# Local attention: the full-row products issued just ahead of the step's first MLP unit, the division ahead of the residual additions

## The chip, the cores and the metric

The kernel runs on one core of a Trainium2 chip. The metric is the device time of one execution in microseconds; the times are medians of several runs. One further execution is recorded by the hardware profiler, and everything that is read from the profile comes from that execution.

## What is computed

Eight sequences of 1024 rows and 256 columns, all in f32, go through two parts, each with a layer norm ahead of it and a residual addition behind it. The first part is a latent attention with 16 heads. The second part is a network of two layers, and the change lies in it:

```python
for l in range(2):
    h = shift_token(x)                       # right half of the columns one row down
    q, k, v = split(h @ wqkv[l])             # 8 heads of 64
    q, k = rotary_xpos(l2norm(q) * qs, l2norm(k) * ks)
    # windows of 128 rows; a query sees its own window and the one before,
    # at most 128 keys back
    o = softmax(mask(8 * q @ k.T)) @ v
    x = x + o @ wo[l]
    h = layernorm(shift_token(x)) * ln_g[l] + ln_b[l]
    a, g = split(h @ w1[l] + b1[l])          # 682 columns each
    x = x + (a * gelu(g)) @ w2[l] + b2[l]
```

## The kernel before, in words

The first part fills the first third of the time, the function `local` the rest. In `local` a pass is one layer of one sequence; there are 16 passes (8 sequences in layer 0, then 8 in layer 1), each of 8 windows of 128 rows, so 128 windows. One loop over steps starts a window per step and runs the parts of earlier windows beside it. The order on PE, DVE, ACT and POOL is the order in which this loop issues (a manual schedule); SP, which issues the DMAs, is ordered by the scheduler.

A step issues, by name: `qk` of this window (PE: 32 matmuls of 512 columns into the tile `pair`; ACT squares; DVE `t1`, `t2`, two operations on `ss`; POOL adds, takes an inverse root and multiplies); `transposes` of the window before (DVE into `turned`, stores to DRAM `z`, and the load `qkT`); `values` of the window four back; `v` of this window (PE: tile `pv`; ACT copies it to `lv`); an output that was held (below); a unit of the MLP; `halves` of the window four back; `scores` of the window three back (PE into `pair`; ACT takes exponentials into `pt`, which POOL masks with one or two selections for each half of the heads); what is left of the MLP's second product (`rests`); `divide` of the window four back (DVE, and for odd windows the DMAs `zo` and `oT`); the output of two windows, every second step; and a second unit of the MLP.

The products of the exponentials with v are made in two parts. `values` (L1068) issues the full-row ones: 128 rows, 32 columns of the array, 65 columns moved, 64 of them (32 for window 0, which has no window before it). `halves` issues, at the same line, those in which only half the rows of a block count. Both add into two PSUM tiles `o`: one has the bank of the pool `pacc`, the other is one of the three banks of the pool `psum3` (tag "mm"), which it holds until `divide` has read it. The other users of these three banks are `pv`, the output's `psw` (L1120, read by the addition at L1124), the MLP's up products `ag` (L724; a gelu on ACT at L1215 reads the gate, a multiplication on DVE at L1216 the other) and its down products `psy`, two tiles, each read by an addition at L1253 (and L1259 in layer 1).

An MLP chunk of 512 rows has eight units and two are run in a step, so the steps repeat in fours. They are named here by their units:

- held step: hidden slices 0 and 1; an output that was held goes ahead of its unit
- middle step: hidden slices 2 and 3; an output at its end
- closing step: hidden slice 4, and the remainder, with statistics and transposes for the next chunk
- sums step: the down products `psy`, 160 matmuls, whose remainder (`rest`, 32 matmuls with 64 rows) and additions follow the scores; then the scaling of the next chunk

Only in the sums step is `rests` filled when the step comes to it. Its output is then put on `held` and issued in the next step. A window with number 2 or 6 starts in a sums step, 3 or 7 in a held step, 0 or 4 in a middle step, 1 or 5 in a closing step.

Within a held, middle or closing step, PE thus runs qk, full-row products, v, (held output), up products, halves, scores, (output), up products.

Of the kernel before, what the change touches and what calls it, by code (L numbers as in the profile page):

```python
# [83 lines left out]
def preln_mla_local_kernel(  # L84
# [627 lines left out]
    def local(ctx: ExitStack, verdict):  # L712
# [39 lines left out]
        def load_attention(l):  # L752


            w = {}
            queue = nc.sync if l else nc.scalar
            w["qkv"] = wa.tile([P, 2, 3 * INNER], F32, tag="qkv", name=f"l_qkv{l}")
            nc.sync.dma_start(w["qkv"], wqkv[l].rearrange("(c p) e -> p c e", p=P))

            for name, src in (("cos", xpos_cos), ("sin", xpos_sin)):  # L760
                w[name] = wa.tile([P, NT, 2, DH], F32, tag=name, name=f"l_{name}{l}")
                queue.dma_start(w[name], src)
                f = wa.tile([P, 2, DH], F32, tag=f"f{name}", name=f"l_f{name}{l}")
                for i, sc_ in enumerate((q_scale, k_scale)):
                    if name == "cos":
                        queue.dma_start(f[:, i, :], sc_[l].partition_broadcast(P))
                    else:
                        queue.dma_start(f[:, i, :H], sc_[l, H:].partition_broadcast(P))
                        queue.dma_start(f[:, i, H:], sc_[l, :H].partition_broadcast(P))
                w[f"f{name}"] = f  # L770
            return w

        def scale_tables(w):
            for name in ("cos", "sin"):
                f = w[f"f{name}"].unsqueeze(1).to_broadcast([P, NT, 2, DH])
                nc.vector.tensor_tensor(w[name], w[name], f, ALU.mult)

        def load_o(l):

            w = wa.tile([P, 4, D], F32, tag="o", name=f"l_o{l}")  # L780
            nc.sync.dma_start(w, wo[l].rearrange("(c p) e -> p c e", p=P))
            return w
# [357 lines left out]
        rests, held = [], []  # L1140
# [135 lines left out]
        def ahead(n):  # L1276
            if n < len(passes):
                l, b = passes[n]
                if n not in streams:
                    streams[n] = stream(b, l)  # L1280
                return next(streams[n])
# [10 lines left out]
        def each(step, name, back):  # L1292
            j = step - back
            if 0 <= j < windows:
                n, i = divmod(j, NT)
                getattr(made[n], name)(i)
# [6 lines left out]
        with tc.manual_schedule(engines={E.PE, E.DVE, E.Activation, E.Pool}):  # L1303
            for step in range(windows + LAG):
                n, i = divmod(step, NT)
                if step < windows and i == 0:
                    l, b = passes[n]
                    if n and b == 0:
                        o = w["o"]
                        w = load_attention(l)  # L1310
                        w["o"] = o
                    made[n] = Pass(n, l, b, w, *ready.pop(n))
                late = step < windows and n and i == 0 and b == 0
                if not late:
                    each(step, "qk", 0)
                each(step, "transposes", 1)
                each(step, "values", 4)
                if not late:
                    each(step, "v", 0)
                while held:  # L1320
                    j = held.pop()
                    made[j // NT].output(j % NT // 2)
                if step >= LAG:
                    next(units, None)
                if NT - 2 <= i and step < windows:
                    ahead(n + 1)
                each(step, "halves", 4)
                if 0 <= step - 3 < windows:
                    nc.scalar.activation(spark, column, AF.Exp)
                each(step, "scores", 3)  # L1330
                full = bool(rests)
                while rests:
                    rests.pop()()
                each(step, "divide", 4)
                if step >= 4 and (step - 3) % LOOK == 0 and step - 4 < windows:
                    inverses = stats.rearrange("p n r h -> p (n r h)")
                    ok = p1.tile([P, INNER], F32, tag="on", name=f"okl{step}")[:, : LOOK * HEADS]
                    nc.vector.tensor_scalar(ok, inverses, 1 / LOW, None, ALU.is_le)
                    nc.vector.scalar_tensor_tensor(ok, inverses, 1 / HIGH, ok, ALU.is_ge, ALU.mult)
                    verdict.add(ok, "local")  # L1340
                j = step - 6
                if 0 <= j < windows and j % 2 == 0:
                    if full and step + 1 < windows:
                        held.append(j)
                    else:
                        made[j // NT].output(j % NT // 2)
                elif 0 <= j < windows - 1 and (j + 1) % (B * NT) == 0:
                    w["o"] = load_o(passes[(j + 1) // NT][0])
                if step >= LAG - 2:
                    next(units, None)  # L1350
                if late:
                    scale_tables(w)
                    each(step, "qk", 0)
                    each(step, "v", 0)
                if i >= NT - 5 and step < windows:
                    got = ahead(n + 1)
                    if got:
                        ready[n + 1] = got
                while rests:
                    rests.pop()()  # L1360
            for _ in units:
                while rests:
                    rests.pop()()
# [519 lines left out]
    with ExitStack() as two:  # L1883
        local(two, verdict)
# [89 lines left out]
```

## Time and profile before

| | |
|---|---|
| median of three runs | 3241.62 us (3237.79 to 3249.9) |
| the profiled execution | 3238.44 us, its span 3236.6 us |
| PE busy | 3082.1 us, 95% |
| DVE busy | 2365.7 us, 73% |
| ACT busy | 1707.0 us, 53% |
| POOL busy | 1375.4 us, 42% |
| full-row products, 128 x 32 array | 7680 matmuls, busy 149.7 us |
| products of half rows | 7680 matmuls, busy 107.1 us |
| division: L1088, L1089, L1096 on DVE | 43.5, 108.6 and 91.1 us |
| additions of psy at L1253 on DVE | 42.7 us for 64 |

A line of a timeline begins with the start and the duration of a group of like instructions in us, then engine, source line, operation, output and input tile, shapes and count; in brackets stands the idle time of the engine before it and what ended it. A line of the waits gives the waiting engine, line and tile, what it waited for, and us in total, times, longest. A line of a table of stretches gives the stretch, its length, the busy time of PE, weight loads (PEld), DVE, ACT and POOL with their counts, PE's granted clock, the share of the DMA engines and GB/s. Matmuls are pipelined: a busy PE may hold products that wait.

### The profile page before, as it was taken

The numbers are of one execution on the slowest core, as the hardware profiler recorded it, in microseconds if no ns is written. First come the engines' busy times: TensorE is split into PE (matmuls) and PEld (weight loads), VectorE is DVE, ScalarE is ACT, GpSimd is POOL, SyncE is SP. The second block draws the span as 40 slices with busy tenths as digits, with TensorE's granted clock in tenths as the row PEclk, the third lists the DMA queues.
The fourth block names the chain that finished last, engine by engine and source line by source line (L and its number), as shares of the span: only waits on it lengthen the run. The fifth ranks groups of instructions, "written<-read, shape, count | busy, mean of one in ns | idle before, by whom it ended". The sixth has DMA issues, their size and how long they took to land. (4 is left out here: it accounts for less than half of the span.)

```text
span 3236.6 us, 124318 instructions
## 1 busy us (share of the span) xinstructions
PE 3082.1 (95%) x55618; PEld 1488.2 (46%) x55618; DVE 2365.7 (73%) x3761; ACT 1707.0 (53%) x2114; POOL 1375.4 (42%) x1070
## 2 busy tenths in 40 slices
PE   7999999999876999999999998999999999999998
PEld 2344444444323555455554444544445455554453
DVE  5999999999875767777676766666666776666652
ACT  6888989888521444444444443334444444444441
POOL 1011111111075655555555554555555555556540
PEclk9999999999998999999999999999999999999999
DMA  5343333333335455554655546555655556565451
GB/s 137 77 103 95 98 101 92 100 93 96 119 109 142 131 163 151 146 158 152 167 141 161 158 133 177 156 155 174 171 156 159 160 158 165 163 177 148 144 154 55
DMA packets 457517, 444.86 MB, mean 137 GB/s; under 512 B 179551, under 2 KB 390926, under 8 KB 456846
## 3 DMA queue, kind: packets, MB, share of 16 engines
q1 hardware_dynamic: 454990, 434.42, 48.2%
q8 instruction: 438, 7.18, 0.9%
q10 hardware_dynamic: 1984, 2.41, 0.2%
q14 instruction: 105, 0.86, 0.1%
HBM read 207.38 MB, written 174.56 MB: 118 GB/s over the span
## 5 line engine op out<-in xcount | busy, mean ns | idle before, releaser
L483 DVE TENSOR_TENSOR pt<-pt,er 128x1024 f32<-128x1024 f32 x576 | 676.0, 1219 | 32.0 <-ACT pt L469 27.0
L724 PE MATMUL ag<-d,l 128*32 128x512 f32 x5632 | 649.7, 595 | 15.1 <-ACT ge L1215 11.1
L958 POOL TENSOR_TENSOR t<-t,t 128x1024 f32<-128x1024 f32 x128 | 303.7, 2373 | 796.4 <-DVE t L954 796.4
L469 ACT ACTIVATE pt<-sc 128x1024 f32<-128x1024 f32 x576 | 560.1, 1029 | 94.2 <-PE sc L461 78.1
L724 PE MATMUL pair<-l_qkv,xT 128*32 128x512 f32 x4096 | 473.0, 595 | 4.4 <-ACT pt L1020 2.6
L1020 ACT ACTIVATE pt<-pair 128x1024 f32<-128x1024 f32 (+1 forms) x256 | 235.5, 968 | 363.7 <-PE pair L1014 357.7
L127 POOL TENSOR_TENSOR rn<-ss,half 128x16 f32<-128x16 f32 x128 | 372.8, 2913 | 13.7
L724 PEld LDWEIGHTS ag<-d,l 128*32 128x32 f32 x5632 | 184.0, 110 | 387.3 <-issue 334.0
L496 PE MATMUL acc<-pt,v 128*32 128x512 f32 (+3 forms) x3072 | 330.7, 500 | 7.4 <-DVE pt L483 7.1
L423 POOL TENSOR_SCALAR_AFFINE_SELECT er<-er 128x128 f32<-128x128 f32 x64 | 74.6, 1175 | 600.9 <-ACT er L421 600.0
L1068 PEld LDWEIGHTS o<-lv,pt 128*32 128x32 f32 (+1 forms) x15360 | 224.4, 108 | 198.3 <-issue 167.3
L949 ACT ACTIVATE sq<-pair 128x1024 f32<-128x1024 f32 x128 | 131.0, 1024 | 347.5 <-issue 326.6
L1216 DVE SCALAR_TENSOR_TENSOR hid<-ag,l_b,ge 128x512 f32<-128x512 f32 x160 | 117.4, 734 | 268.1 <-PE ag L724 175.6
L951 DVE TENSOR_TENSOR t<-pair,l_cos 128x1024 f32<-128x1024 f32 x128 | 155.3, 1213 | 200.7 <-ACT sq L949 200.2
L1120 PE MATMUL psw<-l_o,oT 128*32 128x256 f32 x4096 | 249.7, 395 | 41.8 <-DMA oT<-zo 30.3
L724 PE MATMUL psy<-l,hid 128*32 128x256 f32 x5120 | 284.1, 379 | 0.0
L1068 PE MATMUL o<-lv,pt 128*32 128x65 f32 (+1 forms) x15360 | 256.8, 223 | 20.1 <-POOL pt L1022 12.0
L982 DVE STREAM_TRANSPOSE turned<-t 128x512 f32<-128x512 f32 x256 | 166.0, 685 | 146.1 <-DMA zh<-turnedh 82.4
L724 PEld LDWEIGHTS pair<-l_qkv,xT 128*32 128x32 f32 x4096 | 132.6, 110 | 303.4 <-issue 283.7
L724 PEld LDWEIGHTS psy<-l,hid 128*32 128x32 f32 x5120 | 243.2, 110 | 46.2 <-issue 14.8
L461 PE MATMUL sc<-q,k 32*128 32x512 f32 (+3 forms) x3072 | 248.5, 380 | 12.9 <-DVE x L576 6.8
L724 PE MATMUL pv<-l_qkv,xT 128*32 128x512 f32 x2048 | 252.6, 598 | 0.0
(261 smaller groups left out, 4187.5 us busy)
## 6 DMA issues: line engine op xcount, KB each, us to landing
z<-turned SPq DMA_DIRECT2D x512, 128.0 KB
qkT<-z SPq DMA_DIRECT2D x128, 512.0 KB
zo<-ot SPq DMA_DIRECT2D x256, 128.0 KB
oT<-zo SPq DMA_DIRECT2D x64, 512.0 KB
y<-xs SPq DMA_DIRECT2D x128, 128.0 KB
h<-y SPq DMA_DIRECT2D x32, 512.0 KB
zx<-turneds SPq DMA_DIRECT2D x120, 128.0 KB
xT<-zx SPq DMA_DIRECT2D x240, 64.0 KB
```

The lines of the kernel that those rows point to most:

```text
L127: nc.gpsimd.tensor_tensor(out_, in_, half[:, :n], ALU.pow)
L461: nc.tensor.matmul(two[n // 2][:, n % 2, lo : lo + w], k[rows], q[rows, h], start=(h == 1), stop=(h == 0),)
L469: nc.scalar.activation(pt, sc, AF.Exp, scale=SCALE)
L483: nc.vector.tensor_tensor(t, t, er.to_broadcast([P, 1024 // w, w]), ALU.mult)
L496: nc.tensor.matmul(self.acc[g][32 * n : 32 * n + 32, q0 - c * 512 :], self.v[:, kb, h * VW - at : h * VW - at + 32], pts[n // 2][:, n % 2, ...
L724: nc.tensor.matmul(out[four], w[:, four], rhs, start=start, stop=stop)
L951: nc.vector.tensor_tensor(t1, qk, A[:, i].unsqueeze(2).to_broadcast([P, 2, HEADS, DH]), ALU.mult)
L958: nc.gpsimd.tensor_tensor(t1, t1, t2, ALU.add)
L982: nc.vector.transpose(t[:, :, n], r[:, n])
L1020: nc.scalar.activation(pt[:, :, : n * P], flat[:, :, : n * P], AF.Exp, scale=-1.0)
L1068: nc.tensor.matmul(o[r][32 * c : 32 * c + 32, 2 * g + h % 2, :], self.pts[m][g][rows, place(j), q0 : q0 + 32], self.vs[m][rows, h, :], sta ...
L1120: nc.tensor.matmul(ps[four, i, :], oT[:, (s + 2 * c) % 4, i, c, :], self.w["o"][:, c, :], start=c == 0, stop=c == 3,)
```

## The change

`values` of a step is issued behind `v` and behind a held output, just ahead of the step's first unit, where it stood ahead of both. And `divide` (with the check of its sums, every 32 steps) is issued ahead of the remainder of the down products and their additions, where it stood behind them. No instruction is added or removed.

```diff
                 if not late:
                     each(step, "qk", 0)
                 each(step, "transposes", 1)
-                each(step, "values", 4)
                 if not late:
                     each(step, "v", 0)
                 while held:
                     j = held.pop()
                     made[j // NT].output(j % NT // 2)
+                each(step, "values", 4)
                 if step >= LAG:
                     next(units, None)
...
                 each(step, "scores", 3)
-                full = bool(rests)
-                while rests:
-                    rests.pop()()
                 each(step, "divide", 4)
                 if step >= 4 and (step - 3) % LOOK == 0 and step - 4 < windows:
...
                     verdict.add(ok, "local")
+                full = bool(rests)
+                while rests:
+                    rests.pop()()
                 j = step - 6
```

## The prediction

> **What bounds the kernel now.** The page first, for the engine that carries the time; then the stretch of the local stage in which window steps and MLP units run side by side (1063 to 3094 us).
>
> ```profile
> PE 3082.1 (95%) x55618; PEld 1488.2 (46%) x55618; DVE 2365.7 (73%) x3761; ACT 1707.0 (53%) x2114; POOL 1375.4 (42%) x1070
> ```
> ```profile
> 1063.00:3094.00 2031.00, 1976.46 (x40908) 1020.81 (x40900) 1384.02 (x2486) 873.65 (x1034) 1128.82 (x834) 0.99 0.56 158
> ```
>
> PE is busy for 1976 of 2031 us at a clock of 0.99, so an order that leaves its work as it is can win only PE's waits there: at most some 55 us, and those inside a row of waiting products, which counts as busy. The waits, for this stretch, show which there are:
>
> ```profile
> PEld o L1068 <- POOL pt L1022: 14.0, 39, 1.4
> PE psw L1120 <- DMA oT<-zo: 12.7, 5, 4.8
> PEld ag L724 <- DVE xs L1124: 11.9, 12, 1.0
> PE ag L724 <- ACT ge L1215: 11.1, 14, 0.8
> PE o L1068 <- DVE stats L1088: 4.0, 4, 3.1
> ```
>
> Only the first and the last touch the moved products (o, L1068). The totals of PEld overlap PE's work, so I took the loss from the starts in the timeline. A closing step, and the sums step that follows such a step:
>
> ```profile
> 1927.71 1.10 PE L1068 MATMUL o<-lv,pt 128*32 128x65 f32 x64
> 1928.62 1.90 PE L724 MATMUL pv<-l_qkv,xT 128*32 128x512 f32 x16
> ```
> ```profile
> 1520.26 1.47 PE L1068 MATMUL o<-lv,pt 128*32 128x65 f32 x62
> 1521.03 0.64 POOL L1027 TENSOR_SCALAR_AFFINE_SELECT pt<-pt 128x512 f32<-128x512 f32 x1
> ...
> 1521.56 0.23 PE L1068 MATMUL o<-lv,pt 128*32 128x65 f32 x2
> 1521.62 1.89 PE L724 MATMUL pv<-l_qkv,xT 128*32 128x512 f32 x14
> 1523.26 8.88 PE L724 MATMUL psy<-l,hid 128*32 128x256 f32 x160
> ```
>
> Undisturbed, 64 full-row products take 0.91 us and v 1.72 us (start of pv to start of what follows). In the sums step both take 3.00 instead of 2.63 us: the last products wait for the second mask of the step before, which ends at 1521.67. The step before is the shortest (13.3 us), so POOL has not caught up.
>
> **The change, part by part.** *Nothing added:* the built programs have the same instructions on each engine; PE's order, and with it the PSUM banks, differ, DVE's division and additions are exchanged, ACT and POOL keep their order, and SP's queue swaps one load with two stores, once, near the end of the kernel. So no instruction is priced, only waits.
>
> *Full products behind v (and behind the held output).* They start 1.72 us later (5.17 us in a held step). In the sums step above they would start at about 1521.98, after the mask's end. Reading every step of the stretch in this way (time from the start of qk to pv, less the undisturbed 4.35 us): the 29 sums steps lose 0.33 to 0.38 us each, one of them 2.31, of which 1.72 can be hidden: 28 x 0.36 + 1.72 = 11.8 us. Three of the closing steps lose 0.34: 1.0 us. Middle steps lose nothing. Held steps with window 7 lose 0.03 to 0.73, 5.1 us in twelve steps (one more lost 3.3 us inside qk and one spans the change of layer; both are left out):
>
> ```profile
> 1539.48 0.60 PE L1068 MATMUL o<-lv,pt 128*32 128x65 f32 x26 [0.41 <-POOL pt L1022]
> ...
> 1545.05 1.96 PE L724 MATMUL ag<-d,l 128*32 128x512 f32 x16
> 1547.80 1.92 PE L724 MATMUL ag<-d,l 128*32 128x512 f32 x16 [0.79 <-ACT ge L1215]
> ```
>
> The wait of 0.79 stays: in both programs the second up product of that unit has the bank of the first, and waits for its gelu. Held steps with window 3 gain nothing: there the second up product waits for the addition of psw on DVE, whose chain from the end of qk (square 1.0, t1 1.2, t2 1.3, two ss 2.5, transposes 1.3, addition 0.65, some 0.2 between) is 8.15 us, against 7.8 us of PE's work whatever its order. Sum: 17.9 us.
>
> *What is queued behind, and the covers.* Behind the moved products stands the step's unit, then halves and scores. v's copy on ACT starts earlier, never later. The held output now goes ahead of the products, so a late oT would hold both; but oT lands 8.0 to 14.5 us before that psw in each of the 29 steps, and psw moves up by only 0.9 us. v's bank in the held step now comes from the division of the sums step, psw's and the products' from the two additions behind it.
>
> *Division ahead of the additions.* It acts in sums steps alone, where units leave a rest. DVE stands idle until psy is ready, with the division behind it:
>
> ```profile
> 2816.28 0.69 DVE L1253 TENSOR_TENSOR xs<-psy,xs 128x512 f32<-128x512 f32 x1 [1.44 <-PE psy L724]
> ...
> 2819.38 0.17 DVE L1088 RECIPROCAL stats<-o 128x4 f32<-128x4 f32 x1
> ```
>
> The division needs only halves, which end before scores and rest. Its 1.9 us (two reciprocals 0.17, two multiplications 0.42, a transpose 0.71) move into idle time, of which the waits list 30.7 us in 21 cases. PE waits for that division for only 4.0 us, already in the losses of the held steps, so I add nothing. Where DVE had no idle time (layer 0, window 6: 1533.79 to 1539.7 without a gap), the additions come 1.9 us later instead; the first would end at about 1537.6 and psw, whose bank it frees, starts at 1540.0: 2.4 us of cover. SP's store of xs waits as long, ahead of a qkT load whose scores come two steps later.
>
> *What is late next.* Only psw at the end of a middle step, which waits for oT of the held step before. For window 0 (13 steps in the stretch) the landing precedes its use by 0.1 to 2.4 us, and in five PE waits already (read from the starts: 1.0, 1.5, 1.7, 1.9 and 3.8 us). In layer 0 the chain behind that oT goes through DVE and SP's queue and does not get earlier, so the gain ahead of it (about 0.9 us: 0.36 + 0.43) is lost in two cases wholly and in one by half: +2 us. In layer 1 the chain gets earlier with the division.
>
> *Ahead of 1063 us* there is no MLP, and the products waited 17.0 us in all by the same rows (PE 7.3, PEld 9.7). Bounds: 0, as halves follow at once and oT's landing (11.1 us there) is next, to 4 x 1.72 = 6.9 us for the four steps with a long wait. I take 3, nearer to 0, because those steps end in waits for DMAs.
>
> Sum: -17.9 + 2 - 3 = -19 us (-0.6%). The profiled execution took 3238.44 us (span 3236.6), 3.2 us under the median of 3241.62. 3241.62 - 19 gives 3223 us.
>
> **Rivals.** *Absorbed:* what the products give back is waited for elsewhere, as in the window-3 steps. For it: every held step has a wait behind the products. Against it: in the sums step nothing behind them (psy, halves, scores) waits. It would leave the closing steps and half of what the sums steps lose: -7 us, 3235.
>
> *Slower, by the exchange on DVE.* The additions free the banks of psw and of the products in the held step, and now stand behind 1.9 us of division. Where the first addition ends later than 1.72 us after qk, PE waits. For it: layer 0, window 6, where DVE is full. Against it: the cover of 2.4 us above, and 3.5 us in layer 1. If the cover were missing in 16 held steps the price is 16 x 1.9 = 30 us, less 19: +11, 3253. It decides when DVE runs over 2.4 us later than in this trace.
>
> *Slower, by the clock.* PE gets ahead of oT; a long wait is followed by half clock:
>
> ```profile
> 2142.80 6.56 PE L1120 MATMUL psw<-l_o,oT 128*32 128x256 f32 x64 [3.74 <-DMA oT<-zo]
> ```
> ```profile
> 2141.90:2148.70 6.80, 5.90 (x56) 3.16 (x60) 3.68 (x8) 0.00 (x0) 2.55 (x5) 0.50 0.40 66
> ```
>
> The same psw takes 3.7 us elsewhere; 6.8 us at half clock cost 3.4. The other four waits (1.0 to 1.9 us) kept the full clock, and 0.9 us more leaves them under 3.74. If eight of the 13 went cold: 8 x (3.4 + 0.9) = 34 us, less 19: +15, 3257.
>
> The Trainium skill, "TensorE: Matmul & The Clock Gate", section "HAM oscillation — how this bites in real kernels", has the rule that PE gaps above about 3.4 us cost the clock. The one wait of 3.74 us agrees, the shorter ones do too; by the rule the forecast stands unless a wait for oT grows past that length.
>
> *More:* with DVE earlier, the additions of psw and oT come earlier too: two thirds of the 11.9 us and the 4 us of waits for oT in layer 1 go as well, about -31, 3211.
>
> **Chances.** Forecast 0.70 (its own range 3213 to 3232, from the bounds of the early steps and a few us of PE waits without a releaser that move from run to run); absorbed 0.10; the two slower ones 0.08 and 0.06; more 0.06. A measurement of this kernel can tell 0.5%, 16 us, from no change. Of the forecast's 0.70, 0.51 lies beyond that and 0.19 within; with the rivals: faster 0.57, within 0.29, slower 0.14. The range leaves out the slower cases and the far end of the last: 3204 to 3244.
>
> **What would show it.** Right: in sums steps the products take 0.91 us, none of L1068 waits for POOL pt in the stretch, qk to the unit stays at 6.07 us, the additions (L1253) hardly wait, and the 0.79 us for ge and the 8.15 us chain remain. Wrong: psw waiting for L1253, rows of 0.50 clock at psw, or sums steps as long as before (18.06 and 17.81 us).

## The result and the profile after

The changed kernel takes 3232.45 us (median of 20 runs, 3222.03 to 3246.82) against 3245.79 us for the kernel before in the same comparison (20 runs, 3237.22 to 3262.77): a ratio of 0.9963, 95% interval 0.9949 to 0.9977, so about -12 us (-17 to -7). A second comparison (12 runs, with the experiments below) gave 0.9982 (0.9963 to 1.0001), -6 us. It is faster, by less than the forecast's -19 us. Its profiled execution took 3227.63 us, the span 3225.9.

The page, and the stretch of the step loop in which window steps and MLP units run side by side, cut so that it holds the same 115 steps as the stretch shown of before. The stretch begins at the step that is called the first MLP step here and in the expectations, though the step ahead of it already runs up products:

```profile
PE 3073.7 (95%) x55618; PEld 1406.1 (44%) x55618; DVE 2362.0 (73%) x3761; ACT 1707.8 (53%) x2114; POOL 1371.3 (43%) x1070
```
```profile
1068.90:3083.70 2014.80, 1962.63 (x40904) 935.73 (x40900) 1380.91 (x2488) 873.58 (x1033) 1124.91 (x833) 0.99 0.57 159
```

The same 115 steps took 2030.3 us before (1063.92 to 3094.20) and take 2014.8 us now: 15.5 us less. But the stretch begins at 1068.8 in place of 1063.9, so 4.9 us were lost ahead of it (the expectations say 5.0). Behind it nothing differs (142.4 and 142.3 us). The waits of the stretch that answer to those shown of before:

```profile
PEld ag L724 <- DVE xs L1124: 14.7, 14, 1.3
PE psw L1120 <- DMA oT<-zo: 13.4, 8, 3.4
PE ag L724 <- ACT ge L1215: 12.4, 15, 1.1
PE pv L724 <- DVE on L1089: 3.3, 2, 2.1
DVE stats L1088 <- PE o L1068: 3.0, 6, 1.1
DVE xs L1253 <- PE psy L724: 2.9, 4, 0.9
PEld o L1068 <- POOL pt L1022: 0.5, 1, 0.5
PE o L1068 <- POOL pt L1022: 0.4, 1, 0.4
```

The products' waits for POOL are all but gone (14.0 and 3.6 us before, 0.5 and 0.4 now). The additions, which waited 30.7 us in 21 cases, wait 2.9 us in four. Two of these lines of before, which the prediction does not show:

```profile
PE o L1068 <- POOL pt L1022: 3.6, 7, 1.3
DVE xs L1253 <- PE psy L724: 30.7, 21, 4.4
```

New are two waits of v for the division: v has the bank that the division of the sums step sets free. The waits of psw for oT are more in number (8, were 5).

A sums step behind a closing step, on PE, and the second mask of the step before on POOL:

```profile
1525.64 0.64 POOL L1027 TENSOR_SCALAR_AFFINE_SELECT pt<-pt 128x512 f32<-128x512 f32 x1
```
```profile
1526.59 1.10 PE L1068 MATMUL o<-lv,pt 128*32 128x65 f32 x64
1527.51 8.81 PE L724 MATMUL psy<-l,hid 128*32 128x256 f32 x160
```

The mask ends at 1526.28; the products start 0.31 us later, in one row of 64, and take 0.92 us from start to start. Undisturbed sums steps fell from 18.05 to 17.62 us (window 6) and from 17.81 to 17.39 us (window 2).

In the held step that follows, the gelu's wait is what it was, and in layer 1 the division now stands ahead of the additions on DVE with no gap between them:

```profile
1552.90 1.92 PE L724 MATMUL ag<-d,l 128*32 128x512 f32 x16 [0.79 <-ACT ge L1215]
```
```profile
2806.70 0.14 DVE L1088 RECIPROCAL stats<-o 128x4 f32<-128x4 f32 x1
...
2807.89 0.71 DVE L1096 STREAM_TRANSPOSE ot<-on 128x512 f32<-128x512 f32 x1
2808.53 0.65 DVE L1253 TENSOR_TENSOR xs<-psy,xs 128x512 f32<-128x512 f32 x1
```

### The profile page after: what moved, and what is told of

Same layout as the page of the kernel before. It is cut to its first block, busy times and chain, and to the rows that moved or that the text cites. A ratio compares the mean times of both kernels' runs of the same rounds, so it can differ in the third digit from the quotient of the medians.

```text
span 3225.9 us, 124287 instructions
## 1 busy us (share of the span) xinstructions
PE 3073.7 (95%) x55618; PEld 1406.1 (44%) x55618; DVE 2362.0 (73%) x3761; ACT 1707.8 (53%) x2114; POOL 1371.3 (43%) x1070
## 5 line engine op out<-in xcount | busy, mean ns | idle before, releaser
L724 PE MATMUL ag<-d,l 128*32 128x512 f32 x5632 | 647.6, 594 | 15.2 <-ACT ge L1215 12.4
L724 PEld LDWEIGHTS ag<-d,l 128*32 128x32 f32 x5632 | 176.8, 109 | 348.1 <-issue 294.2
L1215 ACT ACTIVATE ge<-ag,l_b 128x512 f32<-128x512 f32 x160 | 110.1, 688 | 289.3 <-PE ag L724 284.7
L1068 PE MATMUL o<-lv,pt 128*32 128x65 f32 (+1 forms) x15360 | 245.4, 222 | 4.6 <-POOL pt L1022 4.3
```

Source lines behind the costliest of these rows:

```text
L724: nc.tensor.matmul(out[four], w[:, four], rhs, start=start, stop=stop)
L1068: nc.tensor.matmul(o[r][32 * c : 32 * c + 32, 2 * g + h % 2, :], self.pts[m][g][rows, place(j), q0 : q0 + 32], self.vs[m][rows, h, :], sta ...
```

## The experiments

The timed comparisons differ by a few us between runs of one kernel, so each profile was also read in the same way: the start of the first MLP step, the length of the 115 steps from there, and in them the sum of the 29 sums steps, of the 14 held steps with window 7 and of the 14 middle steps with window 0 (from the start of qk to the next start of qk, in us). One of these held steps spans the change of layer (44 us); the middle step behind it counts with 5 us, since its qk is issued at its end. "Ahead" and "behind" tell where the full-row products stand to v in the stretch.

| kernel | products | first MLP step | 115 steps | sums | held, w. 7 | middle, w. 0 | ratio to before (95%) |
|---|---|---|---|---|---|---|---|
| before | ahead | 1063.9 | 2030.3 | 534.9 | 308.7 | 260.2 | 1 |
| division only | ahead | 1067.3 | 2037.1 | 534.2 | 305.8 | 269.2 | 1.0014 (0.9990-1.0037) |
| before, held start | ahead | 1055.8 | 2028.7 | 539.2 | 310.3 | 251.4 | 0.9985 (0.9969-1.0001) |
| held steps only | mixed | 1073.0 | 2049.7 | 540.5 | 305.8 | 274.1 | 1.0019 (1.0002-1.0037) |
| sums steps only | mixed | 1064.4 | 2022.1 | 523.2 | 312.8 | 261.5 | 0.9955 (0.9931-0.9979) |
| sums steps, held start | mixed | 1054.8 | 2027.1 | 523.5 | 313.7 | 258.7 | 0.9938 (0.9915-0.9961) |
| changed | behind | 1068.8 | 2014.8 | 522.3 | 304.8 | 261.7 | 0.9963 (0.9949-0.9977) |
| changed, again | behind | 1069.8 | 2009.9 | 520.9 | 302.9 | 260.5 | 0.9982 (0.9963-1.0001) |
| values only | behind | 1068.0 | 2015.9 | 515.6 | 305.1 | 266.9 | 0.9940 (0.9911-0.9969) |
| changed, old start | behind | 1069.8 | 2012.8 | 521.3 | 303.2 | 261.4 | 0.9956 (0.9925-0.9987) |
| changed, held start | behind | 1056.5 | 2011.4 | 523.2 | 306.2 | 255.8 | 0.9914 (0.9894-0.9934) |
| the same, again | behind | 1057.0 | 2020.9 | 522.3 | 305.2 | 266.1 | 0.9932 (0.9912-0.9951) |
| late output | behind | 1068.1 | 2025.8 | 513.4 | 299.1 | 287.3 | 0.9977 (0.9963-0.9992) |
| late and held | behind | 1063.2 | 2027.1 | 517.6 | 301.4 | 282.0 | 0.9939 (0.9918-0.9959) |

**Values only.** The changed kernel with the division put back behind the additions.

```diff
                 each(step, "scores", 3)
+                full = bool(rests)
+                while rests:
+                    rests.pop()()
                 each(step, "divide", 4)
...
-                full = bool(rests)
-                while rests:
-                    rests.pop()()
```

> Only the full-row products move (behind v and the held output); the division stays behind the residual additions as before. Theory (the whole gain is the products that no longer wait for POOL, the exchange on DVE is worth nothing by itself): all of the change's -12 us is there, the stretch from 1063 us on is 15 us shorter than before, sums steps last 17.6 and 17.4 us, and at most the 4.0 us of PE's waits for the division come back, so -8 to -12 us. Rival (the additions, waiting 30.7 us in 21 cases ahead of the division, hold the division up as soon as the products end later): -2 to -6 us, with PE's waits for the division above 8 us.

Measured: 0.9940, -19 us (-29 to -10); 115 steps of 2015.9 us, the changed kernel's own length. The additions wait ahead of the division as they did before:

```profile
DVE xs L1253 <- PE psy L724: 33.6, 22, 2.8
```

No wait of PE's products for the division is left, though the division is as late as before: the 4.0 us went because the products come later. The rival falls and the theory holds, though its -8 to -12 us lie at the end of the interval. No time here tells this kernel from the changed one.

**Division only.** The reverse: of the change only the second part.

```diff
                 each(step, "transposes", 1)
+                each(step, "values", 4)
                 if not late:
                     each(step, "v", 0)
...
-                each(step, "values", 4)
                 if step >= LAG:
```

> Only the division moves ahead of the additions; the products stay ahead of v. Theory: 0 us, between -4 (PE's waits for the division gone) and +2; PE's 14.0 and 3.6 us of waits of the products for POOL's pt stay, sums steps stay at 18.05 and 17.81 us. Rival (the division's earlier place is what shortens the sums steps): -6 us or more, sums steps at 17.6 us and below.

Measured: 1.0014, +5 us (-3 to +12); sums steps as before (534.2 us). The additions' waits are all but gone, and that is worth nothing that the times show:

```profile
DVE xs L1253 <- PE psy L724: 2.8, 3, 1.8
PE psw L1120 <- DMA oT<-zo: 21.6, 9, 5.1
PEld o L1068 <- POOL pt L1022: 11.7, 33, 1.4
```

**Old start.** The changed kernel, with the products ahead of v in the steps ahead of the first MLP unit (step below LAG).

```diff
                 each(step, "transposes", 1)
+                if step < LAG:
+                    each(step, "values", 4)
...
-                each(step, "values", 4)
+                if step >= LAG:
+                    each(step, "values", 4)
                 if step >= LAG:
```

> The changed kernel, but in the start-up (the steps ahead of the first MLP unit) the full-row products are issued ahead of v as before. Theory (the products behind v end some 1.7 us later, so each pair's division, its store and the load of oT land later, and the steps of the start-up that end in psw wait that much longer: 5.0 us in all): the first MLP step starts near 1064 us instead of 1068.9, and the time is -17 us against the kernel before, 5 us less than the changed kernel. Rival (the 5.0 us are the clock and unexplained waits of one profiled execution): -12 us as with the whole change, and the start of the first MLP step scatters by some us from run to run whatever the order.

Measured: 0.9956, -14 us (-24 to -4), and the first MLP step at 1069.8 us with the old order of the start-up. The start near 1064 us, which my theory asked for, did not come. By the table, the five profiles with the old order there and no held start have it at 1063.9 to 1073.0, mean 1067.7; the four with the new order at 1068.0 to 1069.8, mean 1068.7. The kernel before was profiled with the earliest start of its five.

A part of this scatter lies ahead of anything that an edit touches: the first qk starts at 902.5 us in this profile and at 898.6 in the one before. Counted from the start of the fifth step, the first with products, to the first MLP step, the old order takes 127.5 to 133.5 us (mean 130.0; this kernel 129.1), the new one 131.2 to 132.3 (mean 131.6). So some 2 of the 5 us may belong to the order; one profile of each kernel does not show it.

**Sums steps only, and held steps only.** The kernel before, with the products moved in one kind of step of the stretch alone (here the sums steps; for the held steps the number is 3).

```diff
                 each(step, "transposes", 1)
-                each(step, "values", 4)
+                if step < LAG or step % 4 != 2:
+                    each(step, "values", 4)
                 if not late:
...
+                if step >= LAG and step % 4 == 2:
+                    each(step, "values", 4)
                 if step >= LAG:
```

> The kernel before, with the full-row products moved behind v in the sums steps of the stretch with MLP units alone (28 steps); all else as before, the division behind the additions too. Theory (sums steps 18.05 and 17.81 to 17.62 and 17.39 us, 0.43 us each): -12 us of the stretch's -15.5, and the start-up as before at 1064 us, so -10 to -12 us against the kernel before. Rival (what a sums step gains is waited for in the held step behind it, whose products come 0.4 us sooner after the exponentials): -4 us or less, with longer held steps than 18.82 and 19.51 us.

Measured: 0.9955, -15 us (-22 to -7). In the profile the sums steps give 11.7 us, as the theory has it; the held steps behind them take 4.1 us back (312.8 against 308.7 us, and 313.7 in the kernel with the held start besides), which is a part of the rival. The waits of the products in the stretch, nearly all of them the unmoved ones of the held steps:

```profile
PEld o L1068 <- PE pair L724: 8.7, 6, 1.9
PE o L1068 <- DVE stats L1088: 5.8, 7, 2.4
PEld o L1068 <- POOL pt L1022: 4.0, 8, 0.7
```

> The kernel before, with the full-row products moved behind v and the held output in the held steps of the stretch alone (28 steps, 14 of them with window 7); the division behind the additions. Theory (what the sums steps do not give of the stretch's -15.5 us is here): held steps with window 7 fall from 20.15 us (median) to 19.51, those with window 3 stay at 18.84, so -4 to -6 us against the kernel before; PE's waits of the products for POOL's pt fall by the third that lies in these steps, to about 12 us. Rival (a gain in a held step is waited for at the output of the middle step behind it, where oT lands when it lands): 0 us, with over 16 us of psw's waits for oT.

Measured: 1.0019, +6 us (+1 to +12). The held steps with window 7 gave 2.9 us, in the profile, and the middle steps behind them took 13.9 us (274.1 against 260.2; the three kernels with all products ahead of v have 251.4 to 269.2, so most of this can be scatter), with these waits:

```profile
PE psw L1120 <- DMA oT<-zo: 23.7, 11, 4.2
```

So the rival is nearer: the held steps' part has no gain of its own. In the profiles the two parts are not two gains that add up, for the sums steps' part needs the held steps' part to keep what it wins. The times do not show that: with -15 us, the sums steps alone do as well as the whole change.

**Late output.** The changed kernel with the output of the middle steps issued behind the second unit.

```diff
                     else:
-                        made[j // NT].output(j % NT // 2)
+                        tail.append(j)
...
                 if step >= LAG - 2:
                     next(units, None)
+                while tail:
+                    j = tail.pop()
+                    made[j // NT].output(j % NT // 2)
```

> The changed kernel, with the output of the middle steps issued behind the step's second MLP unit in place of ahead of it (also in the start-up, where there is no unit and the place is the same). Theory (the unit's 3.4 us cover the landing of oT, which came up to 2.7 us after PE was ready): psw's 13.4 us of waits for oT in the stretch from 1063 us fall below 2 us, and the time is -10 to -13 us against the changed kernel, -22 to -25 us against the kernel before. Rival (x, stored 3.4 us later, makes the load of the next rows and the statistics in the closing step late, or the clock drops that follow the long waits go elsewhere): -12 us as with the change alone, with new waits of PE or DVE in the closing and sums steps.

Measured: 0.9977, -8 us (-12 to -3) against the kernel before, so nothing won on the changed kernel. psw's waits for oT are gone, and another wait takes their place:

```profile
PE ag L724 <- ACT ge L1215: 40.5, 29, 2.1
```

One such middle step, on PE and on ACT:

```profile
1714.50 1.92 PE L724 MATMUL ag<-d,l 128*32 128x512 f32 x16
1718.57 3.33 PE L724 MATMUL ag<-d,l 128*32 128x512 f32 x16 [2.15 <-ACT ge L1215]
1721.65 0.67 PE L1120 MATMUL psw<-l_o,oT 128*32 128x256 f32 x4
```
```profile
1716.54 1.28 ACT L1215 ACT_TABLE_LOAD   x1 [0.47 <-PE ag L724]
1717.83 0.69 ACT L1215 ACTIVATE ge<-ag,l_b 128x512 f32<-128x512 f32 x1
```

In this program the second up product of the unit has the bank of the first (with psw ahead of the unit it has another), so it waits for a table load of 1.28 us and the gelu of 0.69 us. This wait of 2.15 us stands in each of the 13 middle steps with window 0 that are not at the change of layer. Behind the one shown the same 16 matmuls take 3.33 in place of 1.92 us. The middle steps with window 0 last 25.6 us more (287.3 against 261.7), of which the sums steps and held steps behind them return 14.6.

**Held start.** The changed kernel, with the start-up's outputs held to the next step.

```diff
-                    if full and step + 1 < windows:
+                    if (full or step < LAG - 2) and step + 1 < windows:
                         held.append(j)
```

> The changed kernel, with the outputs of the start-up (steps ahead of the first MLP unit) held to the next step, behind its v. Theory (the three steps of 23.1 to 24.2 us in the start-up end in waits of 6 to 8 us of psw for oT, which the next step's products then cover): each pair of steps is 4 to 7 us shorter, the first MLP step starts at 1050 to 1057 us instead of 1068.9, and the time is -24 to -30 us against the kernel before. Rival (the start-up is a chain of transfers, of qkT's and oT's round trips, and of the load of the rows of the first MLP unit, whatever PE's order): the wait moves to the first unit or to the scores' wait for qkT, the start stays within 3 us of 1068, and the time is -12 us as with the change alone.

Measured: 0.9914, -28 us (-34 to -21), and the first MLP step at 1056.5 us, 12.3 us earlier than the changed kernel's. Two outputs of the start-up, in the changed kernel:

```profile
978.21 5.71 PE L1120 MATMUL psw<-l_o,oT 128*32 128x256 f32 x64 [7.54 <-issue]
...
1011.03 6.35 PE L1120 MATMUL psw<-l_o,oT 128*32 128x256 f32 x64 [3.44 <-DMA oT<-zo]
```

and with the held start:

```profile
978.42 3.66 PE L1120 MATMUL psw<-l_o,oT 128*32 128x256 f32 x64 [0.84 <-PE pv L724]
...
1007.82 3.63 PE L1120 MATMUL psw<-l_o,oT 128*32 128x256 f32 x64
...
1020.37 2.39 PE L1014 MATMUL pair<-qkT 64*32 64x160 f32 x64 [7.21 <-DMA qkT<-z]
```

They hardly wait, and run in 3.6 us in place of some 6. The longest waits of PE that are left in the start-up are now the scores', for the round trip of qkT and for DVE ahead of it: the chain that the rival named is there, but it left 12 us to be won ahead of it.

> The changed kernel with the outputs of the start-up held to the next step, a second time. Theory (its first time, 0.9914 of the kernel before, was the edit and not the chip): -24 to -30 us against the kernel before, the first MLP step at about 1057 us. Rival: the first measurement was at the edge, -16 to -20 us.

Measured: 0.9932, -22 us (-29 to -16), first MLP step at 1057.0 us. Between the theory and its rival, nearer to the theory. In the same comparison the changed kernel took 0.9982 (0.9963 to 1.0001), and the two intervals lie apart. The medians, 3219.31 us (6 runs) and 3218.16 us (12 runs), are the lowest of the kernels beside 3217.76 us (7 runs) of the sums steps with the held start (below).

**Late and held together.**

> The changed kernel with both the late output of the middle steps and the held outputs of the start-up. Theory: the two gains lie in different stretches and add up, -34 to -43 us against the kernel before (3198 to 3207 us where that takes 3241). Rival (each gain is given back): -12 us.

Measured: 0.9939, -20 us (-27 to -13): neither. The middle steps are nearly as long as with the late output alone (282.0 us), and the start came 6.7 us later than with the held start alone, of which 3.0 us lie ahead of the first products; the rest was not followed further.

**Held start on the kernel before.**

> The kernel before (products ahead of v, division behind the additions), with the outputs of the start-up alone held to the next step. Theory (the start-up's waits of psw for oT are the same in both orders of the products, and holding the outputs covers them in either): the first MLP step starts at 1052 to 1057 us, -10 to -16 us against the kernel before, and nothing else moves. Rival (the gain of the held start needs the products behind v): 0 to -5 us.

Measured: 0.9985, -5 us (-10 to 0); medians 3233.41 and 3242.43. The first MLP step lies at 1055.8 us, as the theory has it, and the 115 steps are as long as before (2028.7 us); but the time is the rival's, and only the end of its interval touches the theory. The profile shows the gain of the start in either order of the products; the times bear out a part of it.

> The kernel before with two edits: the full-row products behind v in the sums steps alone, and the start-up's outputs held to the next step. Theory (of the change only the sums steps count; in the held and closing steps, and in the exchange on DVE, there is nothing): -24 to -28 us against the kernel before, the same as the changed kernel with the held start. Rival (the held and closing steps give the 4 to 7 us that the sums steps left of the profiled -15.5): 4 to 7 us longer than the changed kernel with the held start.

Measured: 0.9938, -20 us (-28 to -13), beside 0.9932 for the changed kernel with the held start on the same chip. The time equals the changed kernel's with the held start, as the theory has it, though -24 us is reached by the interval alone; the profiles show the difference that the rival named (2027.1 against 2011.4 and 2020.9 us for the 115 steps). A time cannot tell 5 us here.

> The changed kernel itself beside the others. Theory: -12 us against the kernel before as measured (0.9963), its first MLP step at 1064 to 1070 us, since the start-up scatters by some us from run to run. Rival (the start-up's 5 us belong to the products behind v): the first MLP step at 1068 to 1069 us again.

Measured: 0.9982, -6 us (-12 to 0), and the first MLP step at 1069.8 us. The place of the start lies in the theory's range and close to the rival's, so it does not decide; the old order gave 1069.8 too (above), so at most a part of the 5 us belongs to the order.

## Why the prediction was right, and where it was not

The sum had three terms. To size them I take means over the profiles: the three with the products ahead of v in all of the stretch (before, division only, before with held start: 115 steps in 2032.0 us) and the six with the products behind it and the outputs in their place (2014.3 us).

- **Products behind v, -17.9 us.** Right. The sums steps gave 15.2 us (predicted 11.8; 28 x 0.43 = 12.0 by the undisturbed steps), the held steps with window 7 gave 3.7 (5.1), those with window 3 gave 1.1 (0), the closing steps nothing (1.0). A little of it is not the products: half clock fills 23.9 us of the 115 steps in the mean of the three profiles and 19.3 in that of the six, and at half speed that is an estimated 2 us. What the sum did not say is that these terms hang together: in the profiles, the sums steps alone lose 4 to 5 us of it in the next step, and the held steps alone lose more than they give.
- **Lost at psw, +2 us.** Its sign and size came, +1.8 us in the middle steps with window 0, with eight waits for oT where there were five; but the same steps differ by 18 us among the three profiles with the products ahead, so the agreement is luck. (The gain ahead of oT, 0.36 + 0.43, is 0.79 and not 0.9; the term stays near 2.) For the stretch the sum predicted -15.9 us; the profiled pair shows -15.5, the means -17.7.
- **Start-up, -3 us.** This is the step that failed. The products' waits there did fall (17.0 to 6.4 us), but three of these steps end in waits of psw (two listed for oT, one with no releaser), and those went from 18.2 to 19.0 us. Nothing was won: between the means the first MLP step moved by +1.0 us, of starts that scatter over 9 us, and by +1.6 us if it is counted from the first products on. That the steps "end in waits for DMAs" stood in the text as a reason for a small term, where it was a reason for none. The held start shows that this end was the bound: move it, and 12 us come off in the profiles.
- **Division, 0.** Right, within what the experiments can tell: where it stands alone it gives nothing (+5 us, -3 to +12), and without it the stretch is as short. The 30.7 us of idle DVE cost nothing.
- **What stays.** The 0.79 us for the gelu stay; held steps with window 3 last 18.83 us as before.
- **Rivals.** Absorbed: not in the whole change, but in the profiles it is what each part shows when it is done by itself. The exchange on DVE: no product of psw waits for L1253; two waits of v for the division, 3.3 us in all, where DVE was full. The clock: two of the middle steps met half clock in the profile after, not eight.

The sum, with 0 in place of -3, is -16, and the means of the profiles give -16.7 (-17.7 + 1.0). The times say -12 (-17 to -7) and -6 (-12 to 0). The first holds the sum at its edge, the second does not, and the two kernels that differ from the changed one by the division or the start-up's order alone gave -19 and -14; the profile is one execution of each kernel, and the stretch of one and the same kernel differed by 9.5 us between two of them. What of the difference is chance is left open. The forecast had most of its chance beyond 0.5%; the change lies within it, at 0.37%.

## What to carry to other kernels

A wait that is removed is worth something only where the engine has nothing to wait for before the end of the step: read what ends the step first, and where that is a transfer, price the removed wait at nothing and move the consumer of the transfer instead. A place in the order does more than hide a wait: it decides who gets which buffer, and the output that was moved out of the way of its transfer made two products share a bank. And a figure read off one execution, such as where a phase starts, needs its scatter before a difference is put down to an edit.

## What was not expected of the hardware

- Waits well below the 3.74 us of the prediction cost the clock. Over the twelve profiles with the output in its old place, the psw of middle steps with window 0 (3.45 us to the start of what follows, undisturbed; the step at the change of layer is left out) took 4.9 us or more behind 10 of the 14 waits of 2.1 to 3.4 us, and behind 7 of the 8 longer ones; behind shorter waits it never took more than 4.8 us. In the profile after, a wait of 2.23 us:

```profile
1428.97 5.35 PE L1120 MATMUL psw<-l_o,oT 128*32 128x256 f32 x64 [2.23 <-DMA oT<-zo]
```
```profile
1429.00:1432.40 3.40, 3.40 (x40) 2.24 (x44) 1.01 (x2) 0.00 (x0) 3.13 (x5) 0.58 0.06 13
```

  The granted clock behind it is 0.58, and psw took 5.14 us to the start of what follows, 1.7 us more than undisturbed. The Trainium skill, "TensorE: Matmul & The Clock Gate", section "HAM oscillation — how this bites in real kernels", puts the length from which gaps bite at about 3.4 us; here the measurement decides, and the bite begins well below.

  What looks like chance above 2 us can be read from the records of the clock. In each of the 14 profiles the clock of the step loop changes on a fixed grid of 3.41 us: half clock lasts 3.41, 6.83, 10.24 or 13.65 us. Cut the 115 steps of each profile along this grid and add up PE's idle time in each piece. Of the pieces at full clock, all 53 with 1.99 us or more were followed by half clock, 6 of the 48 with 1.55 to 1.98 us, and none of the 8088 with less. So it is not the length of a wait that counts in these profiles, but how much of it falls into one piece: in the second profile of the changed kernel a wait of 3.14 us lies with 1.4 us in one piece and 1.8 in the next, and the clock stays at 1.00.

  The profile before has such a case as well, which the prediction did not use, since it looked at the waits for oT alone. Behind this wait at psy the clock is 0.50 for 3.41 us from 1885.91 on:

```profile
1885.42 0.67 PE L724 MATMUL psy<-l,rest_hid 64*32 64x256 f32 x9 [1.84 <-issue]
```
- The switch between the exponential and the gelu on ACT shows as a table load of 1.28 us in the rows. It costs PE nothing as long as PE has a bank to go on with. With the late output it has not, and each of 13 middle steps waits 2.15 us; behind 6 of them half clock follows.
- PE has waits of 0.2 to 3 us with no releaser in the profile ("issue", mostly at psy and at scores) that change places from execution to execution.
